# Pairwise products of an embedding table: a list of 77 output slots, and stores issued from two queues

## The chip, the cores and the metric

The kernel runs on one core of a Trainium2 chip. Five engines of that core matter here: TensorE (PE) multiplies matrices, VectorE (DVE) does elementwise work, and ScalarE (ACT), GpSimd (POOL) and the sync engine (SP) can, among other things, issue DMAs. A DMA is a copy between the chip's large memory and the on-chip memory; 16 DMA engines carry it out, and each of them moves 8 of the 128 partitions of every transfer here. A transfer that an engine's sequencer has issued stands in that sequencer's queue until the DMA engines get to it. When its last byte has landed, a semaphore tells the engines that wait for it.

The metric is device time in microseconds (us), start to end of one execution. The kernel before takes 1287.0 us, the median of three runs (1286.79, 1287.00, 1287.02).

## The reference

`x` has 4096 samples of 32 fields with 64 numbers each, and `W` is 64 x 64. Each field is multiplied by `W`, and for all 496 pairs of fields i < j the product of field i with the transformed field j is written out, element by element:

```python
vid = jnp.einsum('bfd,de->bfe', x, W)
idx_i, idx_j = jnp.triu_indices(32, k=1)
return x[:, idx_i, :] * vid[:, idx_j, :]        # (4096, 496, 64), float32
```

The input has 33.6 MB and the output 520 MB, both in float32. For each number that is read, 15.5 are written.

## The kernel before

**Layout.** The host lays the samples out so that a partition holds one of the 64 numbers for half of the samples, twice over (128 partitions). The 4096 samples make 16 tiles of 2 x 128. One *unit* is 128 numbers in each partition, 512 bytes of a partition. A tile of `x` has 32 units (one a field), and a tile's products have 496 units, so that 16 x 496 = 7936 units are stored in all.

**Memory.** One array `mem` of 445 units holds both inputs and products. `XPLACE` says at which unit each tile of `x` lies. `SLOTS` is a literal list of places for products: (length in units, first unit, and sometimes seams). The products of all tiles follow each other in one long row; slot k takes the next so many of them. Slots overlap in `mem`, with each other and with places of `x` that are no longer needed, so VectorE has to wait before it writes into a slot until the earlier stores from those units have landed, and a load has to wait until stores from its units have landed and the matmuls and products that read them are done. A seam, like a slot's end, cuts an instruction in two, so that its first part need not wait for what only the second part overlaps (`BREAKS`).

**Work.** For each tile, 16 matmuls (L172) write `x @ W` into PSUM, where `vid` has room for one tile: the next tile's matmuls wait for this tile's products. VectorE then writes products (L196), many pairs in one instruction, in the order of `by_block`. When an instruction has filled a slot (`at == end`), the slot's store is issued from the sync engine (L199), one DMA of 128 partitions.

**Loads.** Tile 0 comes with `W` in two DMAs (L136, L140). The others come in groups (`GROUPS`, `CUTS`): tiles 1 to 5 at the start (pieces of 96, 38 and 26 units), then tiles 6 to 10 and tiles 11 to 15, each in pieces of 127, 7 and 26 units, all issued by `load` at L153 from the sync engine. A group is issued behind the store of the slot that was filled when two more tiles were left to do. A *stretch* is the run of stores between two such groups: there are three, and the first follows the *head*, the loads at the start.

**Order.** SP and VectorE run in the order in which the kernel names their instructions (`manual_schedule`). So the sync engine's queue holds, in one order, all 11 loads and all 70 stores. An instruction at its head that waits for a semaphore holds up all behind it. `behind` adds one more wait: the first store after a group of loads is not issued until the last piece but one of that group has landed. ScalarE and GpSimd issue nothing.

Of the kernel before, what the change touches and what calls it, by code (L numbers as in the profile page):

```python
# [26 lines left out]


SLOTS = [
    (96, 221), (120, 80), (116, 200, 21), (100, 64, 16), (92, 164, 36), (92, 256), (127, 96, 68),  # L30
    (124, 223, 33), (125, 64), (120, 191), (64, 311), (112, 79), (124, 224), (108, 64),
    (120, 176, 48), (112, 301), (120, 64), (112, 205), (120, 320), (112, 93), (127, 205), (121, 64),
    (96, 189), (120, 48), (116, 168, 21), (100, 32), (104, 132, 36), (48, 236), (124, 16),
    (127, 157, 79), (109, 0, 16), (120, 109, 48), (88, 229), (127, 16, 93), (127, 160, 69),
    (114, 0, 16), (120, 114), (112, 237), (127, 0), (121, 128), (120, 261), (127, 1), (127, 128),
    (122, 259), (120, 176), (116, 297), (92, 160, 16), (88, 252, 45), (72, 341), (120, 160, 92),
    (120, 293, 48), (32, 413), (120, 173), (126, 319), (122, 144), (127, 287, 32), (119, 128, 16),
    (126, 247), (127, 96), (109, 223), (112, 333), (127, 158), (127, 285), (127, 64, 94),
    (127, 192, 93), (124, 320), (120, 48), (127, 190), (124, 317), (125, 158),
]  # L40


# [10 lines left out]
def by_block():  # L53


    def within(lo):
        yield "step", lo, 2, 1, 0
        for k in range(2):
            yield "step", lo, 4, 2, k
        for i in (lo, lo + 8):  # L60
            yield "row", i + 4, i, 4, 4
        yield "row", lo + 8, lo, 8, 8

    yield from within(0)
    yield "row", 16, 0, 16, 16
    yield from within(16)


def products(blocks, at=0):

    for kind, a, b, c, d in blocks:
        if kind == "row":
            rows, n, i0, di, j0, dj = c, d, b, 0, a, 1
        else:
            rows, n, i0, di, j0, dj = 16 // b, c, a, b, a + c + d, b
        r = k = 0
        while r < rows:
            room = BREAKS[bisect_right(BREAKS, at)] - at
            if k or room < n:
                m, w = 1, min(n - k, room)  # L80
            else:
                m, w = min(rows - r, room // n), n
            yield at, m, w, i0 + r * di + k, di, j0 + r * dj, dj
            at += m * w
            if k + w == n:
                r, k = r + m, 0
            else:
                k += w
# [10 lines left out]
@with_exitstack  # L99
def pairwise_bilinear_kernel(  # L100
    ctx: ExitStack,
    tc: tile.TileContext,
    x0: bass.AP,
    x: bass.AP,
    out: bass.AP,
):

    nc = tc.nc
    NT = sum(len(tiles) for group in GROUPS for tiles in group)
    F = x0.shape[1] - 1 - PAD0
    D = P // 2
    NP = F * (F - 1) // 2

    BANK = 512 // C


    ctx.enter_context(tc.manual_schedule(engines={mybir.EngineType.SP, mybir.EngineType.DVE}))

    const = ctx.enter_context(tc.tile_pool(name="const", bufs=1))
    psum = ctx.enter_context(
        tc.tile_pool(name="ps", bufs=1, space=bass.MemoryType.PSUM)
    )
    vid = psum.tile([P, F, C], F32)

    mem = const.tile([P, UNITS, C], F32)


    w2 = const.tile([P, P], F32)


    place = XPLACE[0]
    nc.sync.dma_start(  # L136
        out=mem.rearrange("p u c -> p (u c)")[:, place * C - D : (place + F // 2) * C],
        in_=x0.rearrange("p u c -> p (u c)")[:, C - D : (1 + F // 2) * C],
    )
    nc.sync.dma_start(out=mem[:, place + F // 2 : place + F, :], in_=x0[:, 1 + F // 2 : 1 + F, :])  # L140
    nc.vector.memset(w2, 0.0)  # L141
    for half in (slice(0, D), slice(D, P)):
        nc.vector.tensor_copy(w2[half, half], mem[half, place - 1, C - D :])  # L143
    loaded = 1

    def load(tiles, cuts=()):
        nonlocal loaded
        n = len(tiles) * F
        place = XPLACE[tiles[0]]
        at = (loaded - 1) * F  # L150
        loaded += len(tiles)
        return [
            nc.sync.dma_start(out=mem[:, place + lo : place + hi, :], in_=x[:, at + lo : at + hi, :])  # L153
            for lo, hi in cuts or [(0, n)]
        ]

    ready = mybir.DependencyInfo(mybir.DependencyClass.Sync, mybir.DependencyReason.DATA)

    def behind(later, earlier):
        tc.add_manual_dep(later.ins, earlier.ins.name, ready, reason="issued when that has landed")  # L160

    pieces = []
    groups, cuts = iter(GROUPS), iter(CUTS)
    for tiles, parts in zip(next(groups)[1:], next(cuts)):
        pieces = load(tiles, parts)

    for t in range(NT):
        xt = mem[:, XPLACE[t] : XPLACE[t] + F, :]


        for b in range(0, F, BANK):
            nc.tensor.matmul(  # L172
                vid[:, b : b + BANK, :],
                lhsT=w2,
                rhs=xt[:, b : b + BANK, :],
                start=True,
                stop=True,
            )

        for at, m, w, i, di, j, dj in products(by_block(), t * NP):  # L180
            slot = bisect_right(STARTS, at) - 1
            n = m * w
            begin, end = STARTS[slot], STARTS[slot + 1]
            ot = mem[:, SLOTS[slot][1] : SLOTS[slot][1] + SLOTS[slot][0], :]
            o = ot[:, at - begin : at - begin + n, :]
            if m == 1:
                left = xt[:, i : i + w, :]
                right = vid[:, j : j + 1, :].to_broadcast([P, w, C])
            else:
                o = o.rearrange("p (m w) c -> p m w c", m=m)  # L190
                right = vid[:, j : j + (m - 1) * dj + 1 : dj, :].unsqueeze(2).to_broadcast([P, m, w, C])
                if di == 0:
                    left = xt[:, i : i + w, :].unsqueeze(1).to_broadcast([P, m, w, C])
                else:
                    left = xt.rearrange("p (m d) c -> p m d c", d=di)[:, i // di : i // di + m, i % di : i % di + w, :]
            nc.vector.tensor_tensor(o, left, right, ALU.mult)  # L196
            at += n
            if at == end:
                store = nc.sync.dma_start(out=out[:, begin:end, :], in_=ot)  # L199
                if pieces:  # L200
                    behind(store, pieces[-2])
                    pieces.clear()


        if t + 2 == loaded < NT:
            (tiles,) = next(groups)
            pieces = load(tiles, next(cuts))


_INS = ["r_x", "L0_rec_W"]  # L210
# [42 lines left out]
```

## Time and profile before

| | |
|---|---|
| median of 3 runs | 1287.0 us |
| the profiled execution | 1287.24 us |
| its span, first to last instruction | 1285.5 us |
| VectorE busy, 348 instructions | 1084.0 us, 84% |
| TensorE matmuls busy, 256 instructions | 231.1 us, 18% |
| weight loads busy | 67.7 us, 5% |
| moved by DMA | 553.75 MB, mean 431 GB/s |
| DMAs from the sync engine's queue | 11 loads, 70 stores |
| issue to landing of a store, least / median / most | 19.6 / 24.6 / 38.1 us |

The page of the profile cuts the span in 40 equal slices (32.1 us each) and gives for each the busy share of every engine in tenths, the busy share of the 16 DMA engines, and the rate. Waits are listed as "who waited for whom", with the total, the number and the longest. The chain of waits goes back from the last instruction to what released it, and on to the start. Each line names the kernel's line (L196) and the arrays, output first (`mem<-mem,vid`); "SPq" is the sync engine's sequencer. Behind the page lie records of single packets: for each, the start, the time it took, its bytes and its queue. One packet of data is one partition's part of a DMA, here called a row. Besides the program's own queue, the trace has a few packets of two more queues, which fetch instructions.

### The profile page before, as it was taken

How to read it: one execution, taken by the hardware profiler on the slowest of the kernel's cores; microseconds unless marked ns; L12 is line 12 of the kernel's file. 1: busy time of each engine (PE TensorE's matmuls, PEld its weight loads, DVE VectorE, ACT ScalarE, POOL GpSimd, SP SyncE). 2: the span in 40 equal slices, each digit the busy share in tenths (PEclk: the TensorE clock that was granted, in tenths of full speed). 3: DMA queues.
4: the chain of work that ended last, by engine and by line, in shares of the span. 5: the costliest groups of instructions: out<-in, count | busy, mean ns of one | idle time of the engine just before them, and what ended most of it. 6: DMA issues, size and time to landing. Idle time of an engine off the chain costs nothing.

```text
span 1285.5 us, 1143 instructions
## 1 busy us (share of the span) xinstructions
PE 231.1 (18%) x256; PEld 67.7 (5%) x256; DVE 1084.0 (84%) x348; POOL 0.2 (0%) x4
## 2 busy tenths in 40 slices
PE   5031121303120212040311211103122130312000
PEld 1000000100000000010000000000000010000000
DVE  6889998899967389899799992849998889999952
POOL 0000000000000000000000000000000000000000
PEclk8555565556555556555565555556555555555555
DMA  9999999999999999999999999999999999999998
GB/s 400 438 429 438 436 428 438 431 435 436 432 430 439 416 433 425 445 430 433 439 427 441 435 429 436 419 432 429 440 432 440 429 430 441 429 441 430 434 436 370
DMA packets 11670, 553.75 MB, mean 431 GB/s; under 512 B 1296, under 2 KB 1296, under 8 KB 1552
## 3 DMA queue, kind: packets, MB, share of 16 engines
q1 hardware_dynamic: 11664, 553.69, 99.8%
q8 instruction: 2, 0.03, 0.0%
q14 instruction: 4, 0.03, 0.0%
HBM read 33.59 MB, written 520.09 MB: 431 GB/s over the span
## 4 chain that ended last, share of the span: by engine, by line
DVE 47%; DMA 44%; issue 6%; PE 0%; DVEq 0%; SPq 0%
DVE mem L196 47%; DMA out_dram<-mem 41%; DMA mem<-in_r_x_dram 3%; PE vid L172 0%; DVEq L241 0%; DVEq L196 0%; DVE w L143 0%; SPq L153 0%; DVEq L143 0%; SPq L199 0%
## 5 line engine op out<-in xcount | busy, mean ns | idle before, releaser
L196 DVE TENSOR_TENSOR mem<-mem,vid 128x1024 f32<-128x1024 f32 (+17 forms) x345 | 1083.4, 3212 | 170.5 <-DMA out_dram<-mem 164.2
L172 PE MATMUL vid<-mem,w 128*128 128x512 f32 x256 | 231.1, 1039 | 951.3 <-DVE mem L196 843.8
L172 PEld LDWEIGHTS vid<-mem,w 128*128 128x128 f32 x256 | 67.7, 306 | 1113.5 <-DVE mem L196 1011.9
L143 DVE COPY w<-mem 64x64 f32<-64x64 f32 x2 | 0.4, 190 | 5.0 <-DMA mem<-in_r_x_dram 4.9
L141 DVE MEMSET w<- 128x128 f32 x1 | 0.2, 165 | 0.8 <-PEq L221 0.8
L221 POOL MEMSET const-bfloat16-1.0<- 128x1 bf16 x1 | 0.1, 101 | 0.0
L221 POOL MEMSET const-uint8-127<- 128x1 uint8 x1 | 0.1, 101 | 0.0
L221 POOL MEMSET const-float32-0.0<- 128x1 f32 x1 | 0.1, 98 | 0.2 <-issue 0.2
L221 POOL MEMSET const-float32-1.0<- 128x1 f32 x1 | 0.1, 98 | 0.0
## 6 DMA issues: line engine op xcount, KB each, us to landing
out_dram<-mem SPq DMA_DIRECT2D x15, 8128.0 KB, 27.4
out_dram<-mem SPq DMA_DIRECT2D x14, 7680.0 KB, 24.9
out_dram<-mem SPq DMA_DIRECT2D x6, 7168.0 KB, 26.2
out_dram<-mem SPq DMA_DIRECT2D x5, 7936.0 KB, 28.2
out_dram<-mem SPq DMA_DIRECT2D x3, 7424.0 KB, 22.6
out_dram<-mem SPq DMA_DIRECT2D x3, 5888.0 KB, 20.9
mem<-in_r_x_dram SPq DMA_DIRECT2D x2, 8128.0 KB, 37.6
out_dram<-mem SPq DMA_DIRECT2D x2, 8064.0 KB, 24.3
```

The lines of the kernel that those rows point to most:

```text
L141: nc.vector.memset(w2, 0.0)
L143: nc.vector.tensor_copy(w2[half, half], mem[half, place - 1, C - D :])
L172: nc.tensor.matmul(vid[:, b : b + BANK, :], lhsT=w2, rhs=xt[:, b : b + BANK, :], start=True, stop=True,)
L196: nc.vector.tensor_tensor(o, left, right, ALU.mult)
L221: nc = _bacc.Bacc("TRN2", target_bir_lowering=False, num_devices=1, dynamic_dma_scratch_size=512)
```

## The change

The list of slots is another one, of 77 in place of 70, with the same 7936 units in all. Its slots are shorter on the average (103 units against 113), the shortest stand after the groups of loads, and fewer have seams. Places of `x`, groups and cuts are as before.

The stores no longer all go out from the sync engine. A counter, `turn`, starts at 0 with each group of loads. The first four stores of a stretch (turn 0 to 3) are issued from the sync engine, and from then on ScalarE and the sync engine take turns, ScalarE first (turn 4, 6, 8...). The first store of a stretch waits, as before, for the last piece but one of the loads; the fifth, ScalarE's first, for the last piece. ScalarE joins the engines that keep the order written in the kernel.

```diff
 SLOTS = [
-    (96, 221), (120, 80), (116, 200, 21), (100, 64, 16), (92, 164, 36), (92, 256), (127, 96, 68),
...
+    (88, 229), (88, 64), (88, 152, 77), (76, 241), (88, 64), (96, 152), (100, 248), (108, 64, 88),
+    (108, 172, 76), (68, 281), (108, 64), (108, 172), (100, 281), (124, 64, 108), (124, 188),
+    (68, 313), (124, 64), (120, 188), (104, 308), (124, 64), (124, 188), (127, 317), (125, 64),
+    (96, 189), (84, 32), (80, 116, 73), (88, 197), (84, 32), (80, 117), (88, 197), (100, 0),
...
+    (88, 100), (96, 188), (96, 0), (104, 100, 88), (104, 208), (96, 0), (112, 96), (104, 208),
+    (120, 0), (112, 120), (112, 237), (126, 0), (122, 128), (127, 254), (121, 0), (120, 134),
+    (112, 269), (120, 197), (96, 317), (56, 160, 37), (56, 216), (64, 277, 40), (72, 341),
...
+    (127, 190), (127, 318), (122, 64), (120, 198), (127, 318), (124, 40), (125, 164),
 ]
...
-    ctx.enter_context(tc.manual_schedule(engines={mybir.EngineType.SP, mybir.EngineType.DVE}))
+    ctx.enter_context(tc.manual_schedule(engines={mybir.EngineType.SP, mybir.EngineType.DVE, mybir.EngineType.Activation}))
...
+    turn = 0
     for t in range(NT):
...
             if at == end:
-                store = nc.sync.dma_start(out=out[:, begin:end, :], in_=ot)
-                if pieces:
-                    behind(store, pieces[-2])
-                    pieces.clear()
+                queue = nc.scalar if turn > 3 and turn % 2 == 0 else nc.sync
+                store = queue.dma_start(out=out[:, begin:end, :], in_=ot)
+                turn += 1
+                if pieces and turn in (1, 5):
+                    behind(store, pieces[-2] if turn == 1 else pieces[-1])
+                    if turn == 5:
+                        pieces.clear()
 
 
         if t + 2 == loaded < NT:
             (tiles,) = next(groups)
             pieces = load(tiles, next(cuts))
+            turn = 0
```

## The prediction

> **What bounds the kernel now.** I read the page's slices first, because the four engines together say little when one resource is full from end to end.
>
> ```profile
> DVE  6889998899967389899799992849998889999952
> ...
> DMA  9999999999999999999999999999999999999998
> GB/s 400 438 429 438 436 428 438 431 435 436 432 430 439 416 433 425 445 430 433 439 427 441 435 429 436 419 432 429 440 432 440 429 430 441 429 441 430 434 436 370
> DMA packets 11670, 553.75 MB, mean 431 GB/s; under 512 B 1296, under 2 KB 1296, under 8 KB 1552
> ...
> q1 hardware_dynamic: 11664, 553.69, 99.8%
> HBM read 33.59 MB, written 520.09 MB: 431 GB/s over the span
> ```
>
> The DMA engines are busy in every slice and one queue holds 99.8% of their time; VectorE has gaps. So the time is bytes over rate, plus whatever the DMA engines lose. The packet records of the trace give the loss. A row (one partition's share of a DMA) of 127 units, 65,024 bytes, takes 2.399 us and one of 7 units (3,584 bytes) 0.140 us: 0.0082 us for each row, and beyond that 27.2 GB/s per engine. All rows at the large rows' rate take 553.68 MB / 434 GB/s = 1275.8 us of the span of 1285.5. The other 9.7 us are the head (the first rows start at 1.74 us and are small), the end (the last landing is at 1284.6 and differs by 2.9 us between DMA engines), and five changes between loads and stores, 2.7 us together by the rows that took longer than their size, some 0.55 each.
>
> How close to dry does the queue run? The chain of waits shows it:
>
> ```profile
> 1000.32 24.54 DMA out_dram<-mem
> 1024.86 0.03 issue
> 1024.89 0.02 DVEq L196
> 1024.91 0.04 issue
> 1024.95 12.62 DVE mem L196 x4
> 1037.58 0.02 issue
> 1037.60 24.23 DMA out_dram<-mem
> ```
>
> A store issued at 1000.32 lands 24.54 later though its bytes are 19.1 us: it was issued 5.4 us ahead of the landing before it. By the landing records the smallest such lead is 5.0 us, and no store lost time by it. A row needs about 1.0 us from issue to start (0.73 to 1.74 for the first DMA) and lands 0.36 us after its end. Three more views: VectorE's waits, SP's own waits (us in total, times, longest), and the groups of products with shapes kept apart (busy us, mean ns, idle before):
>
> ```profile
> DVE mem L196 <- DMA out_dram<-mem: 164.2, 33, 21.8
> ```
>
> ```profile
> SPq L199 <- DVE mem L196: 1104.4, 67, 32.5
> SPq L199 <- DMA mem<-in_r_x_dram: 96.8, 3, 35.8
> ```
>
> ```profile
> L196 DVE TENSOR_TENSOR mem<-mem,vid 128x8192 f32<-128x8192 f32 x26 | 225.5, 8680 | 22.6 <-DMA out_dram<-mem 22.6
> L196 DVE TENSOR_TENSOR mem<-mem,vid 128x1024 f32<-128x1024 f32 x101 | 117.4, 1212 | 39.9 <-DMA out_dram<-mem 33.6 <-PE vid L172 6.2
> ```
>
> VectorE waits 164 us for memory that a store still holds. It needs 1.13 us for 8 units against 1.21 us of DMA (0.151 us a unit), so it can't win back much: a slot that comes free late makes the next store late.
>
> **The change, part by part.** *Bytes and products.* Unchanged: both lists cover 7936 units plus the same padding. VectorE's total of 1084 us stays within a few us (seams and slot ends cut some products anew at about 0.07 us per extra cut, 1212 against half of 2279), hidden under 1285 us of DMA; it would show only where the lead is near nothing.
>
> *Seven more stores.* 8 rows per DMA engine each at 0.0082, and a semaphore row of 0.009: 7 x 0.075 = 0.5 us, on the path, since the DMA is the path. The issue itself (0.33 us on SP) is hidden by the lead. ScalarE ran nothing before, so nothing stands behind its waits but its own stores.
>
> *Two queues instead of one.* This is the part that decides, and before has one program queue only. What it does show is a second queue's single row: instruction fetches of 8 KB. The one at 151.24 us starts when a store's row ends (151.247) and that store's next row starts as it ends (151.550): it went in between two rows of one store, not after the store. So I take two queues as alternating row by row on each engine. The Trainium skill, page "DMA: Bandwidth & Descriptors", section "Queues, rings and completion order", says that an engine turns between queues only after a packet, of about 9 to 17 descriptors; a store's share is 8 rows and a semaphore write, which by that rule would go whole, in order of issue, and by it the sum would be 1287.5. The row contradicts it here, at least for a waiting single row, and I go by the row. The same page ("Issuing engines are not separate DMA queues") says that spreading over issuing engines saves issue time alone; no rate gain is in my sum either.
>
> *What alternation does to leads.* Write S1, S2... for the new stores. S1 to S4 (88, 88, 88, 76 units) go in order after the head, whose last load lands at 33.9 in the trace: landings at 47.2, 60.5, 73.8 and, alone, 85.3. S5 is ScalarE's (88 units at 64, over S2's place): VectorE starts at 60.5, needs 11.5 to 12 us, issue at 72.5. Its rows arrive as S4's begin, so they alternate: 164 units x 0.151 = 24.8 us, both done at 98.3, S4's last row one row (1.7 us) earlier, landed at 97.0 instead of 85.3. S6 (96 units at 152) ends at unit 248 and S4 lies from 241: its last 12 units wait for S4, then two products of 1.1 and 0.6 us: issue at 98.7, first row at 99.7. The engines are empty from 98.3: 1.4 us lost. In order, S6 would be issued at 87, 11 us ahead. S7 and S8 then have leads near 2.5 us, just enough. In the second stretch the same pair (88 units at 197, fourth on SP; 84 at 32 from ScalarE) lands together some 11 us late, and the two stores that need those places have leads of about 1.5 us; I put 1.0 there (0 where the drift between engines covers it). The third stretch's small slots (56, 56, 64) leave 12 us. Sum of stalls 2.4; lower bound 0 (in order, all leads 11.5 or more), upper 5, if the drift of up to 3 us makes the short leads dry too.
>
> *Loads beside ScalarE's stores.* Before, the pieces at L153 follow the last store in one queue:
>
> ```profile
> 387.73 2.89 SPq L153 DMA_DIRECT2D mem<-in_r_x_dram  x3
> ...
> 446.94 12.35 DVE L196 TENSOR_TENSOR mem<-mem,vid 128x1408 f32<-128x1408 f32 x2 [21.77 <-DMA out_dram<-mem]
> ```
>
> They were issued 18.2 us ahead, behind a store of 121 units; one change of direction. After, the second group (units 285 to 445) waits for the store at 317, on SP, while ScalarE's store of 125 units at 64 is in flight with about 5 of its 8 rows left; those would alternate with 5 load rows. The third group is alike (store at 134 on SP, 112 units at 269 on ScalarE). That is about 8 more changes each, 16 in all, or 8 read rows put between writes. Four instruction fetches, reads between store rows, lengthened their neighbours by 0.64, 0.35, 0.29 and 0.36 us, mean 0.41: 8 x 0.41 = 3.3 us. The other bound is the five changes of before, when all engines turn together: 16 x 0.55 = 8.8. Below, 0, if loads beside stores cost nothing once they run. I take 3.3, since a read among writes from another queue is the nearer row. ScalarE's first store after a load waits for the last piece; by the ledger that has long landed (33.9 against 72.5), so this wait costs nothing, and its cover is the 38 us between.
>
> **Sum.** 0.5 + 2.4 + 3.3 = 6.2. The profiled execution is 1287.24 with a span of 1285.5, which becomes 1291.7; the median is 1287.0, which becomes 1293.2. From the bounds: 0.5 + 0 + 0 to 0.5 + 5 + 8.8, so 1287.5 to 1301.3.
>
> **Rivals.** *In order.* If an engine takes a store's whole share before it turns, leads are 11.5 us or more everywhere, no load mixes with a store, and only 0.5 us is added: 1287.5. For it: the slot list, read in order of issue, never lets the lead fall under 11.5 except behind loads; against it, the fetch at 151.24. *Rows alternate but mixing is free:* 1287.0 + 0.5 + 2.4 = 1289.9. *Faster.* The 0.0082 us per row may be a gap that one queue's rows can't hide and a second queue's can. Of 704 rows on each engine some two thirds stand in stretches with both queues filled: 470 x 0.0082 = 3.9 us, less the 0.5: 1283.6. It decides only if leads hold too. For it: the overhead is the same for every size; against it: rows already start 3 ns before the last ends, and the fetch's neighbours got longer. *The list is not what it says:* not so; the build order has 34 of 77 stores on ScalarE's queue.
>
> **Chances.** Forecast (alternation with stalls and mixing, 1289.7 to 1299): 0.60. Mixing free: 0.09, about its half over the bound. In order: 0.21. Faster: 0.10. About 0.2%, 2.6 us, is what a measurement tells from no change. Slower 0.65, same 0.25, faster 0.10. The range 1286.5 to 1298.5 leaves out the faster case and the upper tail.
>
> **What would show it.** Right: packets of both queues interleaved row by row with twice the time from issue to landing (about 30 to 40 us in place of 24.6); a dip in GB/s near 98 us and a VectorE wait there for the fourth store; load rows slowed around 385 to 405 and 800 to 820. Wrong: landings about 18 to 25 us apart in issue order, no VectorE-caused gap, loads that begin only when ScalarE's last store has ended; or row times of 2.39 or less per 65,024 bytes.

## The result, and the profile after

| | before | after |
|---|---|---|
| median of 8 runs of each | 1286.82 us | 1291.22 us (1289.77 to 1292.11) |
| the profiled execution, and its span | 1287.24, 1285.5 | 1292.11, 1290.3 |
| VectorE busy, instructions | 1084.0 us, 348 | 1082.0 us, 311 |
| DMAs from SP, from ScalarE | 81, 0 | 54, 34 |
| issue to landing of a store, least / median / most | 19.6 / 24.6 / 38.1 | 16.1 / 30.3 / 41.8 |

The changed kernel takes 1.0033 times as long [1.0023, 1.0044], 4.4 us more. Its profiled execution is the longest of its eight, 0.9 us over the median, and what follows from its trace adds up to that one.

The slices and DMA parts of the page of after:

```profile
DVE  6969989989973669998999973768989899889890
...
DMA  9999999999999999999999999999999999999998
GB/s 399 432 430 426 419 433 435 437 448 432 438 420 400 442 430 417 439 439 433 431 421 441 440 437 417 410 431 434 437 435 433 434 435 438 422 438 426 432 439 386
DMA packets 12678, 553.75 MB, mean 429 GB/s; under 512 B 1408, under 2 KB 1408, under 8 KB 1664
...
q1 hardware_dynamic: 7776, 315.40, 56.8%
q10 hardware_dynamic: 4896, 238.29, 42.9%
HBM read 33.59 MB, written 520.09 MB: 429 GB/s over the span
```

Two queues now share the work, the bytes are the same, and still no slice of the DMA engines shows a gap: a slice is 32 us long, and what was lost is some us in all, spread over few places. The slices can't find them; the chain of waits does. After, from 59 us on (start, duration, what):

```profile
59.15 36.03 DMA out_dram<-mem
95.18 0.03 issue
95.21 0.02 DVEq L197
95.23 0.04 issue
95.28 18.04 DVE mem L197 x8
```

The store issued at 59.15 is S4 (76 units). It needs 36.03 us where the prediction's ledger had 26 for it alone. VectorE can't go on before it has landed, at 95.18. The timeline of after shows what then follows (start, duration, instruction; in brackets the idle time before it and what ended it):

```profile
83.03 2.35 DVE L197 TENSOR_TENSOR mem<-mem,vid 128x1024 f32<-128x1024 f32 x2
...
95.28 31.73 DVE L197 TENSOR_TENSOR mem<-mem,vid 128x1024 f32<-128x1024 f32 x11 [9.91 <-DMA out_dram<-mem]
...
97.12 28.58 SPq L201 DMA_DIRECT2D out_dram<-mem  x2
...
110.72 0.34 ACTq L201 DMA_DIRECT2D out_dram<-mem  x1
```

VectorE sits idle for 9.91 us, then finishes S6, which SP issues at 97.12; S7 follows from ScalarE at 110.72. Why did S4 land so late? The records of single packets say it. They don't name the DMA engine; the rows of one engine are found by each one's starting within some 5 ns of where the last one ends. One such chain (start us, us, bytes, queue; q1 is SP's, q10 ScalarE's; a record of 4 bytes is the write that signals the semaphore):

```
82.923 1.665 45056 q10
84.584 1.439 38912 q1
86.019 1.665 45056 q10
87.681 1.439 38912 q1
89.116 1.665 45056 q10
90.777 1.439 38912 q1
92.212 1.665 45056 q10
93.874 0.009     4 q1
93.879 1.665 45056 q10
95.541 1.665 45056 q10
97.202 0.009     4 q10
97.951 1.851 49152 q1
```

The engine takes one row of S4 (38,912 bytes) and one of S5 (45,056), in turn. Rows have their usual lengths, so nothing is slower as such. But S4, which lands at 85.13 when the list runs from one queue (below), lands here 10 us later, and S5 is no earlier for it (98.51, against 98.41 from one queue). S4's last row ends at 92.216, and its signal still waits for a row of S5. From 97.211 to 97.951 the engine has no row at all: S6 was issued too late to be there.

**Where the time went.** For each trace I added up, over all rows, the time beyond a row's size (0.0082 us plus its bytes at 27.2 GB/s, the prediction's formula), and the time without a row between 10 and 1278 us, as means over the 16 DMA engines:

| us | before | after |
|---|---|---|
| rows by their size | 1277.56 | 1278.02 |
| rows beyond their size | 4.16 | 8.04 |
| without a row | 0.05 | 1.67 |
| mean end of the engines' last rows | 1282.07 | 1287.85 |
| end of the last engine's | 1284.27 | 1289.03 |

The means end 5.78 later; the first three lines add up to 0.46 + 3.88 + 1.62 = 5.96, a little more, since a row starts some 3 ns before the one ahead of it has ended. The last engine ends only 4.76 later, since the 16 engines finish closer together than before: that gave 1.0 back.

### The profile page after: what moved, and what is told of

Same layout as the page of the kernel before. It is cut to its first block, busy times and chain, and to the rows that moved or that the text cites. A ratio compares the mean times of both kernels' runs of the same rounds, so it can differ in the third digit from the quotient of the medians.

```text
span 1290.3 us, 1127 instructions
## 1 busy us (share of the span) xinstructions
PE 230.5 (18%) x256; PEld 67.7 (5%) x256; DVE 1082.0 (84%) x311; POOL 0.2 (0%) x4
## 4 chain that ended last, share of the span: by engine, by line
DMA 54%; DVE 37%; issue 6%; PE 0%; DVEq 0%; SPq 0%
DMA out_dram<-mem 49%; DVE mem L197 37%; DMA mem<-in_r_x_dram 5%; PE vid L173 0%; DVEq L246 0%; SPq L153 0%; DVEq L197 0%; DVE w L143 0%; SPq L201 0%; DVEq L143 0%
## 5 line engine op out<-in xcount | busy, mean ns | idle before, releaser
L197 DVE TENSOR_TENSOR mem<-mem,vid 128x1024 f32<-128x1024 f32 (+13 forms) x308 | 1081.4, 3584 | 169.7 <-DMA out_dram<-mem 163.4
```

## The experiments

Each ratio is to the kernel before in the same series (medians 1286.6 to 1286.8), with a 95% interval. "Theory" is the prediction's: stalls through row-by-row alternation, and loads that mix with stores. Sums called row excess are those of the table above, by the same formula.

**The list alone.** All stores from SP, with the old wait.

```diff
-                queue = nc.scalar if turn > 3 and turn % 2 == 0 else nc.sync
+                queue = nc.sync
...
-                if pieces and turn in (1, 5):
-                    behind(store, pieces[-2] if turn == 1 else pieces[-1])
-                    if turn == 5:
-                        pieces.clear()
+                if pieces:
+                    behind(store, pieces[-2])
+                    pieces.clear()
```

> The new list of 77 slots, every store and load from the sync engine. Theory (the loss comes from two queues that alternate row by row): the leads are 11.5 us or more, nothing mixes, and only the seven more stores remain, 0.5 us: ratio 1.0004 to the kernel before, 1286.8 to 1288; the rows that took longer than their size add up to 6 us (before 6.05, after 10.39), no idle near 98, 498 and 512 us. Rival A (the list itself costs the time, by shorter slots or more VectorE waits): 1290.5 to 1291.5, ratio 1.003, with the same dips near 98 and 385 us.

Measured: 1287.24 us, ratio 1.0005 [0.9996, 1.0015]; row excess 4.25, without a row 0.04. (The 6.05 and 10.39 of the expectation were counted in another way; by the table's formula they are 4.16 and 8.04.) The mean end is 1282.52, 0.45 after that of before, which the 0.46 of 56 more rows account for. The same stretch in this kernel's chain of waits:

```profile
48.79 24.86 DMA out_dram<-mem
...
74.35 10.83 DVE mem L197 x3
85.18 0.04 issue
85.22 15.42 DVE mem L197 x6
100.64 0.02 issue
100.66 27.37 DMA out_dram<-mem
```

VectorE goes from one product to the next from 74 to 100 us. So the list is not the cause. Its windows against those of after (stretch; length, busy us and instructions of PE, PEld, DVE and POOL; TensorE's clock; DMA share; GB/s):

```profile
95.00:100.00 5.00, 0.45 (x1) 0.45 (x2) 5.00 (x2) 0.00 (x0) 0.50 0.99 427
100.00:105.00 5.00, 3.34 (x4) 0.73 (x3) 5.00 (x3) 0.00 (x0) 0.50 0.89 383
```

```profile
90.00:95.00 5.00, 0.00 (x0) 0.00 (x0) 0.00 (x0) 0.00 (x0) 0.50 1.00 433
95.00:100.00 5.00, 3.26 (x4) 1.00 (x4) 4.72 (x4) 0.00 (x0) 0.50 0.92 395
100.00:105.00 5.00, 0.89 (x2) 0.00 (x0) 5.00 (x2) 0.00 (x0) 0.50 0.75 324
```

The first two lines are the list's alone, the last three after's. Over 95 to 105 us the rates' means are 405 and 360 GB/s: 0.45 MB less in 10 us, about 1.0 us at 434 GB/s. That is rough, since this view puts a whole row where it starts: the list alone shows 383 GB/s in a window in which its engines have rows throughout. The packet records give 0.87 us without a row in after at 95 to 100, and none in the list alone. At 90 to 95 after's VectorE does nothing while the DMA engines are still full: the wait itself costs nothing there, what it makes late does.

**No store beside a load.** In the changed kernel the two stores that were in flight when loads came go out from SP; every other store stays where it was.

```diff
-                queue = nc.scalar if turn > 3 and turn % 2 == 0 else nc.sync
+                queue = nc.scalar if turn > 3 and turn % 2 == 0 and slot not in (22, 47) else nc.sync
```

> The changed kernel, but the last store before each later group of loads (slots 22 and 47) goes out from the sync engine, so that no store of ScalarE's is in flight beside a load. Theory: the long rows at 384 to 393 and 804 to 812 us (1.9 us a group, against 0.58 in the kernel before) go back to about 0.6, the stalls near 98 and 512 stay: 2.6 us less than the changed kernel, 1288 to 1289.3, ratio 1.0015. Rival B (mixing is harmless and the stalls cost all): 1291 as before. Rival C (loads and the fourth store aside, two queues cost in every row): 1290 or more.

Measured: 1290.48, ratio 1.0027 [1.0016, 1.0037]. That is 0.7 under the changed kernel, with intervals that overlap; the forecast gain isn't there. The rows of both load groups and of the stores around them do show it: 3.93 us beyond their size in the changed kernel, 2.19 here. But two other stores' rows, at 496 to 512 us, grew by 0.7, and the engines end further apart.

**ScalarE begins four stores later.**

```diff
-                queue = nc.scalar if turn > 3 and turn % 2 == 0 else nc.sync
+                queue = nc.scalar if turn > 7 and turn % 2 == 0 else nc.sync
```

> The changed kernel, but the first eight stores of a stretch, not four, go out from the sync engine, so that the fourth and the sixth no longer share the DMA engines with the fifth. Theory: by the ledger the lead of the sixth store goes from under 0 to about 11 us, the idle and the long first rows near 98, 112, 498 and 512 us (2.6 us together) go, the load groups stay as they are: 1288 to 1289.5, ratio 1.0015. Rival D (the stall only moves to where ScalarE now starts): 1290.5 to 1291.5 with a new dip near 150 to 170 us.

Measured: 1289.38, ratio 1.0025 [1.0017, 1.0034]. The eleven times lie in two groups, six from 1288.89 to 1289.38 and five from 1290.89 to 1291.55, so the median says little; the profiled execution (1289.08) is of the shorter ones. In it the dip at 90 to 100 us is gone, but in the third stretch it comes back at another place. The chain of waits and the windows of this kernel there:

```profile
905.28 36.12 DMA out_dram<-mem
...
950.12 23.14 DVE mem L197 x11
```

```profile
950.00:955.00 5.00, 1.35 (x2) 0.50 (x2) 5.00 (x5) 0.00 (x0) 0.50 0.97 418
955.00:960.00 5.00, 2.80 (x3) 0.50 (x2) 5.00 (x3) 0.00 (x0) 0.50 0.84 357
```

There 0.94 us are without a row, all but 0.02 of this kernel's total: again the store ahead of ScalarE's first one lands 36 us after its issue. A stall by alternation belongs to no fixed place: it comes where ScalarE's first store shares with one that VectorE needs soon.

**Both.** `turn > 7` and slots 22 and 47 from SP.

```diff
-                queue = nc.scalar if turn > 3 and turn % 2 == 0 else nc.sync
+                queue = nc.scalar if turn > 7 and turn % 2 == 0 and slot not in (22, 47) else nc.sync
```

> Both edits: eight stores on the sync engine first, and slots 22 and 47 from the sync engine; 25 stores or so still go out from ScalarE in turn. Theory: nothing is left but the seven more stores, the same as with one queue, 1286.8 to 1288, ratio 1.0004 (up to 0.8 us more, for a shorter lead where ScalarE starts). Rival C (row-by-row turns cost something in themselves): 1289 or more. Rival E (two queues gain rate where nothing stalls): below 1286.

Measured: 1289.70 (1286.88 to 1290.24), ratio 1.0017 [1.0008, 1.0026]; forecast were 1286.8 to 1288. Here too the times lie in two groups, four from 1286.88 to 1287.41 and seven from 1289.30 to 1290.24. The profiled execution, 1287.12, is of the shorter ones: it has 0.09 us without a row and a row excess of 5.01, so what makes the median longer can't be read from it, and it stays open. What the shorter ones show is that 26 stores from ScalarE need not cost anything: they take as long as the list from one queue.

**The old list from two queues.** The kernel before with the new turns and the new wait.

```diff
-                store = nc.sync.dma_start(out=out[:, begin:end, :], in_=ot)
-                if pieces:
-                    behind(store, pieces[-2])
-                    pieces.clear()
+                queue = nc.scalar if turn > 3 and turn % 2 == 0 else nc.sync
+                store = queue.dma_start(out=out[:, begin:end, :], in_=ot)
+                turn += 1
+                if pieces and turn in (1, 5):
+                    behind(store, pieces[-2] if turn == 1 else pieces[-1])
+                    if turn == 5:
+                        pieces.clear()
```

> The old list of 70 slots with the new turns between queues (the change without its list). Theory: the old list gives leads of 5 to 8 us where the new one gives 11.5, and a store that shares with its neighbour lands some 10 us late, so the queues run dry: by the ledger idle of 2.4 to 4.9 us at four places or so, 13 us, and some ten leads under 4 us at 0.5 each: 1300 to 1306, ratio 1.012. Rival (the leads don't matter, mixing does): 1290 to 1292.

Measured: 1304.26, ratio 1.0136 [1.0122, 1.0149], as expected. 8.8 us are without a row between 10 and 1278 us (3.0 of them at 520 to 530), and the row excess is 10.24. Its chain of waits:

```profile
495.81 26.59 DMA out_dram<-mem
...
524.76 16.82 DVE mem L197 x5
541.58 0.02 issue
541.60 27.14 DMA out_dram<-mem
```

A store lands, VectorE fills the next slot for 17 us, and that store starts. Where slots come free only just in time in order of issue, sharing makes waits of them. The new list, whose leads are 11 us or more, absorbs most of it.

**Eight stores from ScalarE, far from any need.** Each has a lead of 6.8 us or more in the ledger of landings, shared rows counted.

```diff
-                queue = nc.scalar if turn > 3 and turn % 2 == 0 else nc.sync
+                queue = nc.scalar if slot in (18, 20, 43, 50, 52, 71, 74, 76) else nc.sync
```

> The new list; eight stores (slots 18, 20, 43, 50, 52, 71, 74, 76) go out from ScalarE's queue, the others from the sync engine. They are chosen, with the store times of 0.151 us a unit, so that when each of them and its neighbour share the DMA engines the next stores still have leads of 6.8 us or more, and no load is beside one. Theory (two queues cost only by short leads and by loads beside stores): no more than the list in one queue, 1286.6 to 1287.8, and no row far over its size at these stores. Rival C (turning between queues costs in itself): these eight stretches of about 16 rows per engine show longer rows, 1288.5 or more.

Measured: 1287.11, ratio 1.0002 [0.9993, 1.0011], row excess 4.23 against 4.25 for the list alone. From its page:

```profile
q1 hardware_dynamic: 11520, 498.05, 89.8%
q10 hardware_dynamic: 1152, 55.64, 10.0%
...
HBM read 33.59 MB, written 520.09 MB: 431 GB/s over the span
```

A tenth of the time goes to a second queue and the rate is that of before. Turning between queues costs nothing here that can be measured, and gains nothing. The latter agrees with the Trainium skill, page "DMA: Bandwidth & Descriptors", section "Issuing engines are not separate DMA queues".

**Loads from ScalarE, stores in order.** The list alone, with the two later groups of loads issued from ScalarE.

```diff
-            nc.sync.dma_start(out=mem[:, place + lo : place + hi, :], in_=x[:, at + lo : at + hi, :])
+            (nc.scalar if loaded > 6 else nc.sync).dma_start(out=mem[:, place + lo : place + hi, :], in_=x[:, at + lo : at + hi, :])
```

> The new list with every store from the sync engine, but the two later groups of loads from ScalarE's queue, so that the one thing left of the change is a load that starts beside a store in flight. Theory: the entry of each group costs 1.9 us a DMA engine in place of 0.8 with one queue, and the change back to stores less, so +1 to +3 us on the list in one queue (1287.2): 1288.2 to 1290.2, and more if the first store after the loads then comes late. Rival B (mixing harmless, all of the loss is in the leads): 1286.8 to 1287.6.

Measured: 1290.38, ratio 1.0030 [1.0020, 1.0041]. It looks like a price of mixing, and isn't a clean one. The timeline of this kernel:

```profile
825.79 26.61 DVE L197 TENSOR_TENSOR mem<-mem,vid 128x8192 f32<-128x8192 f32 x4 [25.19 <-DMA out_dram<-mem]
...
834.50 22.78 SPq L201 DMA_DIRECT2D out_dram<-mem  x3
```

Loads that alternate with stores make those stores land late; VectorE waits 25.19 us for one, and the first store behind the third group is issued at 834.50. 1.80 us are without a row, 1.29 of them just before. The rows of the load groups themselves took only 0.75 us more beyond their size than with the list alone (3.02 against 2.27), though an engine changes between load and store rows 12 and 11 times at the two groups, and 2 and 2 times with the list alone (means over the chains of rows).

**No wait behind the loads.** The kernel before without `behind`.

```diff
-                if pieces:
-                    behind(store, pieces[-2])
-                    pieces.clear()
```

> The kernel before without the wait of the first store of each stretch for the loads: that store is queued behind them as soon as VectorE has filled its slot. If the longer load rows at the change from loads to stores (0.58, 0.47 and 0.34 us a DMA engine) come of a store's being issued while the last load rows run, they go: 1 us less, 1285.5 to 1286. If they come of the change of direction itself, no difference: 1286.6. It may beat both kernels.

Measured: 1287.24, ratio 1.0003 [0.9995, 1.0012]; row excess 4.09 against 4.16. The rows at the change from loads to stores got longer, those at the change from stores to loads shorter. The wait that the change rearranges is worth nothing that can be measured here.

**Mixing without short leads.** ScalarE has only stores around the two load groups, so that rows of loads and stores alternate there as in the changed kernel; all else from SP.

```diff
-                queue = nc.scalar if turn > 3 and turn % 2 == 0 else nc.sync
+                queue = nc.scalar if slot in (20, 22, 43, 45, 47) else nc.sync
```

> The new list; only slots 20, 22, 43, 45 and 47 go out from ScalarE's queue. By the ledger every lead stays at 7 us or more (but at the first stores after the loads, as with one queue), and at both later groups of loads a store of ScalarE's is in flight for 17 us or more beside them: loads beside stores are left alone of the change. Theory, by the changed kernel's rows (3.95 us over their size about the two groups, 2.33 with the list in one queue): +1.6 us on the list in one queue, 1288.3 to 1289.3, ratio 1.0017. By the prediction's price, 0.41 for each load row between store rows: +3.3, 1290.5. Rival B (mixing harmless): 1287.2.

Measured: 1287.27, ratio 1.0005 [0.9997, 1.0014]. The load groups' row excess is 2.54, 0.27 more than for the list alone; 0.17 us are without a row. Loads between stores of another queue cost nothing that shows in the time. The packet records of after show why (one chain, columns as above; 64,000 bytes are a row of the 125-unit store, 65,024 of the 127-unit load):

```
386.041 2.361 64000 q10
388.399 2.758 64000 q10
391.153 3.326 65024 q1
394.475 2.361 64000 q10
396.833 2.399 65024 q1
399.228 2.361 64000 q10
401.586 2.399 65024 q1
```

Only the entry is slow: one store row and one load row, 1.32 us together beyond their size. From then on the direction changes with every row, and every row has its usual length.

**The fifth stores alone.** Only ScalarE's first store of the first stretch and that of the second (slots 4 and 27) go out from ScalarE; 2 stores in place of 34.

```diff
-                queue = nc.scalar if turn > 3 and turn % 2 == 0 else nc.sync
+                queue = nc.scalar if slot in (4, 27) else nc.sync
```

> The new list; only slots 4 and 27, the fifth stores of the first two stretches, go out from ScalarE's queue, so that of the change only the two late landings of the fourth stores are left. Theory: idle near 98 us, long first rows near 98, 112, 498 and 512 us, 2.4 to 2.8 us in all, no mixing: 1289.3 to 1290.3, ratio 1.0022. Rival (the stalls are made good later, or mixing is all): 1287.2 to 1288.

Measured: 1289.52, ratio 1.0023 [1.0014, 1.0032]; 1.21 us without a row, 1.09 of them at 90 to 100 us. Its chain of waits, and then its ScalarE queue and windows:

```profile
59.20 36.04 DMA out_dram<-mem
95.24 0.03 issue
95.27 0.02 DVEq L197
95.29 0.04 issue
95.34 17.98 DVE mem L197 x8
```

```profile
q10 hardware_dynamic: 288, 11.27, 2.0%
```

```profile
95.00:100.00 5.00, 3.20 (x4) 1.00 (x4) 4.66 (x4) 0.00 (x0) 0.50 0.84 357
100.00:105.00 5.00, 0.95 (x2) 0.00 (x0) 5.00 (x2) 0.00 (x0) 0.50 0.80 344
```

The chain is that of after to within 0.1 us, with 2.0% of the DMA time on the second queue. Two moved stores cost 2.3 us against the list alone, over half of the change's 4.4. In this trace the engines' last rows end 2.67 later in the mean than with the list alone (1285.19). 1.17 of it are engines without a row, nearly all at the first place; 1.50 are rows beyond their size, of which 0.57 and 0.58 lie in the first and the second stretch, spread over the stores behind the late one at a few ns a row. Why these rows are longer isn't shown.

One part of the expectation failed: the long first rows near 112, 498 and 512 us aren't there. S7 begins 1.83 us after its issue, as in after (1.81), but from the sync engine, like S6 before it, and its first rows take 0.00 us beyond their size; in after, from ScalarE, they take 0.85.

No version ran faster than the kernel before; four can't be told from it: the list alone, the eight far apart, mixing alone, and the old one without its wait.

## Why the prediction was right, and which term was off

*Direction and mechanism.* Slower was forecast, by alternation with stalls and mixing; 1293.2 against 1291.22 measured. The mechanism of the stalls stands as written: row-by-row turns, S4 late through S5, S6 through S4, empty engines near 98 us. That the sum came within 2 us is in part luck: the term for mixing was twice what the trace has, longer rows that it didn't have came in, and 1 us was given back at the end.

*Two queues alternate row by row.* Right, and it was read from one instruction fetch. The rule of the Trainium skill, page "DMA: Bandwidth & Descriptors", section "Queues, rings and completion order", that an engine turns only after a packet of some 9 to 17 descriptors, would have S4's 8 rows and its signal go whole: by it S4 lands near 85 and the change costs 0.5 us. The records show a turn after every row of 38 to 65 KB, and S4 at 95.18. Here the measurement decides against the page.

*The stall near 98 us.* Forecast: S4 landed at 97.0, S6 issued at 98.7, first row at 99.7, 1.4 us lost. Measured: 95.18, 97.12 and 97.95, with 0.87 us without a row. Two errors cancel in part: S5 started later than assumed (its first row at 76.7 while S4's began at 71.5, so S4's first rows went alone), and S4's signal took 2.0 us in place of 0.36. But S7, called "just enough" at 2.5 us, wasn't: it was issued 2.5 us ahead of S6's landing, as forecast, its first rows began 1.81 us after its issue, and the store took 0.86 us beyond its size. By the fifth stores alone this is not the short lead as such, but a short lead on the other queue than the store before it. The second stretch has 0.67 without a row, and the two stores behind its late landing (slots 29 and 30) 0.25 more row excess. So the stalls come to 0.87 + 0.67 + 0.79 + 0.25 = 2.6 us of DMA time (0.79 is the row excess of ten stores from S6 on; both above the list alone), against 2.4. The other stores of the second stretch have 0.53 more, a few ns a row, whose cause isn't shown.

*Seven more stores.* 0.5 forecast; 0.46 by the rows' sizes, and 0.45 in the mean end with the list alone.

*The fifth store's added wait.* It cost nothing, as said: the last piece landed at 33.83, and the store was issued at 72.85.

*Loads beside stores.* This is the step that was mis-sized: "8 x 0.41 = 3.3 us". In the changed kernel the two load groups, with the stores around them, took 3.93 us beyond their size, 1.66 more than with the list alone. The count was wrong: not "16 in all" more changes of direction, but 5.5, since an engine changes 6.1 times in the mean at the second group of loads and 3.4 times at the third, and 2 times each with the list alone. And the price goes with the entry, not with each change: the last row before the first change and the first behind it took together 1.8 us beyond their size at each group, against 0.75 and 0.89 with the list alone, and all other rows there no more than with the list alone. An instruction fetch that lengthens its neighbours is no model for a steady mix: the loads from ScalarE made 19 changes more for 0.75 us. Mixing alone cost 0.27 in rows and 1287.27 against 1287.24 in time. Of the rivals, "mixing is free" was thus nearer on this part, and its 1289.9 is 1.3 under the result where the forecast is 2.0 over it.

*What wasn't in the sum.* The engines ended closer together, which gave 1.0 us back in the profiled execution. Rows a few ns longer behind the late stores cost some tenths of a us in a stretch.

*What stays open.* The fifth stores alone explain 2.3 of the 4.0 us between the list alone and the changed kernel. For the other 1.7 the traces point to S7 and its kind, to load entries, to more empty engines in the second stretch, and to rows a few ns longer; how they divide isn't settled, since the experiment without mixing took only 0.7 off and that isn't resolved. Nor is it why the load entries of the changed kernel (3.93 with the stores around them) are slower than where mixing stands alone (2.54); each was seen in one trace. Nor is it what parts the two groups of times, some 2 us, in the two kernels with `turn > 7`.

## What to carry to other kernels

When the DMA engines are the bound and slots are reused, ask of every store not how long it takes but who waits for it: here a second queue left the rate as it was, and where two stores shared the engines, the earlier landed some 10 us late, and the later no sooner. Before stores are spread over queues, redo the ledger of landings with shared rows, and where a store is issued late, look on which queue the store before it is: in these runs a first row that began under 3 us after its issue was long only on the other one. Price a suspected cost by a kernel that has it alone; here the changed kernel's rows around the loads looked like 1.7 us, and alone it was nothing that showed.

## What the runs showed of the hardware that wasn't expected

- **A store's signal lags with two queues.** From the end of its last row to the semaphore it took 0.36 us in one queue (median of before); where two alternate, mostly 2.2 to 2.8 us (after). In the records of S4 above the signal takes its turn behind a row of the other queue.
- **A short lead is paid on the other queue, even if nothing runs dry.** Where a store followed one of the other queue and its first row began 1.1 to 2.95 us after its issue on busy engines, its first rows took 0.44 to 0.89 us beyond their size in 14 of 18 cases, over five runs (S7: 1.81 and 0.85), and at most 0.17 in the other four. Behind a store of its own queue they took at most 0.03 in all 35 cases of 1.1 to 3 us, 19 of them in the kernel before. From 3 us on nothing was seen on either queue (at most 0.03). In the changed kernel's three cases with empty engines the first row came 0.83 us after issue and took 0.05 to 0.09 beyond its size.
